# Outer product of routed experts: weights stationary instead of slots, with a turn back, in an eight-expert layer of a twelve-step network

## The chip, the cores and the metric

The kernel runs on one core of a Trainium2 chip. The metric is the time of one launch on the device in microseconds (us). A core has five engines that work from queues of their own: TensorE (PE; its weight loads are shown as PEld), VectorE (DVE), ScalarE (ACT), GpSimd (POOL) and SyncE (SP, which only starts transfers here). An engine takes its instructions strictly in order: an instruction that waits for a semaphore holds up everything behind it on its engine. All data here is fp32.

## The reference

Twelve steps work one after another on x, 4096 tokens of 128 numbers. Each adds a function of the normalised x to x:

```python
    x = L0_attn_x
    x = x + 0.5 * _L0_ffn_ref(_layernorm(x, axis=-1), ...)
    x = x + _L0_attn_ref(_layernorm(x, axis=-1), ...)
    x = x + 0.5 * _L0_ffn_ref(_layernorm(x, axis=-1), ...)
    x = x + 0.5 * _L1_ffn_ref(_layernorm(x, axis=-1), ...)
...
```

The layers L1, L2 and L3 follow in the same manner (ffn, attention, ffn). The change lies in `_L0_ffn_ref`, which is called twice. It is a layer of eight experts of which each token takes the two that its router prefers. Seven experts are real; the eighth only scales the token. Each real expert takes at most 512 tokens ("slots"):

```python
        cap = math.ceil(n_tok / n_exp * CAPACITY_FACTOR)
        logits = jnp.einsum('bsh,eh->bse', x, router_w) + router_b
        weights_flat = jax.nn.softmax(logits, axis=-1).reshape(n_tok, n_exp)
...
        inputs = inputs.reshape(cap, n_exp - 1, hidden)
        in_w = jnp.take_along_axis(expert_w, sorted_indices, axis=0)
        h = jax.nn.relu(jnp.einsum('ceh,ehi->cei', inputs, experts_inter))
        out = jnp.einsum('cei,eih->ceh', h, experts_out) * in_w[..., None]
        combined = jnp.zeros_like(x_flat).at[used_idx].add(out.reshape(-1, hidden))
        combined = combined + x_flat * (noop_w * noop_mask)[:, None]
```

So for each real expert there is an inner product, 512 slots x 128 by 128 x 512, then a relu, then an outer product, 512 slots x 512 by 512 x 128, then a factor for each slot, and then the slot's row is added to its token.

## The kernel before

**Stages.** `l0_block` runs the two feed-forward steps and the attention of layer 0. Each feed-forward step has three stages: routing (softmax, ranks within the experts, and two tables of row numbers, `src` and `dst`), the expert loop `experts` (L656), and the return, in which the experts' rows are read back and added to x (`returned`, L473). Routing stores the normalised tokens with their eight routing weights behind them as rows of 136 numbers in `xd`, in device memory. The first call of `experts` (L889) stands between the routing and the return with the attention; the second (L911) ends the block.

**Device memory.** Each call has an array of its own, `yds[n]`, with two rows for each token, one for each of its choices, and spare rows for empty slots. Rows that no expert writes must be zero, so `zeros(n)` (L464) writes them first: four transfers of 1 MB each, started by SyncE, from the tile z, which GpSimd fills with zeros once, at the kernel's start (L447). `zeros(0)` is issued among the weight loads. `zeros(1)` belongs to the second call and is issued in the first.

**The loop.** For each expert e of 7, with tiles of 128 partitions:
- fetch(e, s), s of 4: GpSimd gathers 128 rows of xd into the tile g (L664; four buffers, so four experts). Slots lie on partitions.
- turn(e): four transposes on TensorE (L676) put g's 128 columns on partitions, in gp; VectorE copies gp to gt (L678).
- inner(e): four matmuls (L684), for each a block of 128x128 of w1 stationary and gt's 512 columns (slots) moving. The results hp go through two PSUM banks; the relu to h is on VectorE for the odd ones (L686), on ScalarE for the even ones (L688). So h has the inner dimension on partitions and slots in columns.
- outer(e): 16 matmuls (L694): for each of four blocks of 128 slots, four blocks of the inner dimension are summed up in op. A block of h is stationary, and 128 columns of w2 move. The result has slots on partitions again, so the routing weight is one number per partition: ScalarE scales op to y with it, one activation for each block of slots (L697). y has three buffers.
- put(e, s): GpSimd scatters 128 rows of y into yds[n] (L668).

Three experts are fetched ahead of the loop. Then, for each e: inner(e), turn(e+1), outer(e), the four puts of e interleaved with the four fetches of e+3, and then the side work that falls to e.

**What sets the order.** Both calls run in a stretch in which the order of the program is the order of the instructions on TensorE, ScalarE and VectorE; in the first call also on SyncE (L887, L906). Elsewhere a planner places instructions. On GpSimd the order comes out as 16 gathers (experts 0 to 3), then put(0), fetch(4), put(1), fetch(5), put(2), fetch(6), and the puts of 3 to 6.

**Side work.** The list `beside` is spread over the seven experts: work k of m is done behind expert 7k // m. In the first call it is zeros(1), eight times self_part (four VectorE operations at L654: the eighth expert's share), and the loading of layer 1's weights (`l1_ffn_weights`, L990 to L1013, small loads on SyncE with some VectorE work; the first reader of one of them on another engine is at L1006). In the second call it is self_part in turn with eight steps that multiply layer 3's two weight matrices with each other (L1865, four matmuls of 128 columns into pp, and a ScalarE copy at L1866) and with small sums on VectorE for layer 2 (L1626, L1628). PSUM is shared by tags: "mm" (gp, op) and "hp" have two banks each, "f3" (pp) one.

**SyncE's queue in the first call.** zeros(1)'s four transfers stand first, then loads for later layers, then the loads r of yds[0] (L482), which wait for the scatters.

Of the kernel before, what the change touches and what calls it, by code (L numbers as in the profile page):

```python
# [8 lines left out]
F32 = mybir.dt.float32  # L9
I32 = mybir.dt.int32  # L10
AF = mybir.ActivationFunctionType
# [5 lines left out]
P = 128  # L17
NB = 8
# [126 lines left out]
class Net:  # L145
# [316 lines left out]
        return w  # L462

    def zeros(self, n):  # L464
        for k in range(4):
            self.nc.sync.dma_start(
                out=self.yds[n][2048 * k : 2048 * k + 2048, :].rearrange("(p n) d -> p (n d)", p=P), in_=self.z)
# [24 lines left out]
    def l0_block(self, w):  # L492
# [6 lines left out]
        nc, tc, a = self.nc, self.tc, self.a  # L499
        box = {}  # L500
        with ExitStack() as c:
# [149 lines left out]
            def self_part(b):  # L651
                for i in range(4):
                    t, x = 4 * b + i, self.x[b][:, i, :]
                    nc.vector.scalar_tensor_tensor(x, self.xn[b][:, i, :], box["pw"][:, t, 7:8], x, ALU.mult, ALU.add)  # L654

            def experts(wk, ps, n, beside):  # L656

                src, dst, yd = box["src"], box["dst"], self.yds[n]
                gs, gts, hs, ys = {}, {}, {}, {}

                def fetch(e, s):
                    if s == 0:
                        gs[e] = wk.tile([P, 4, P + 8], F32, tag="g", name="g", bufs=4)
                    nc.gpsimd.indirect_dma_start(  # L664
                        out=gs[e][:, s, :], out_offset=None, in_=self.xd[:, :], in_offset=bass.IndirectOffsetOnAxis(ap=src[:, e, s : s + 1], axis=0))

                def put(e, s):
                    put = nc.gpsimd.indirect_dma_start(  # L668
                        out=yd[:, :], out_offset=bass.IndirectOffsetOnAxis(ap=dst[:, e, s : s + 1], axis=0), in_=ys[e][:, s, :], in_offset=None)

                    self.apart(f"puts{n}", put.ins)

                def turn(e):
                    gp = ps.tile([P, 512], F32, tag="mm", name="gp")
                    for s in range(4):
                        nc.tensor.transpose(gp[:, s * P : (s + 1) * P], gs[e][:, s, 0:P], self.ident)  # L676
                    gts[e] = wk.tile([P, 512], F32, tag="gt", name="gt")
                    nc.vector.tensor_copy(gts[e], gp)  # L678

                def inner(e):  # L680
                    h = hs[e] = wk.tile([P, 4, 512], F32, tag="h", name="h")
                    for ic in range(4):
                        hp = ps.tile([P, 512], F32, tag="hp", name="hp")
                        nc.tensor.matmul(hp, lhsT=w["w1"][:, e, ic * P : (ic + 1) * P], rhs=gts[e], start=True, stop=True)  # L684
                        if ic % 2:
                            nc.vector.tensor_scalar(h[:, ic, :], hp, 0.0, None, ALU.max)  # L686
                        else:
                            nc.scalar.activation(h[:, ic, :], hp, AF.Relu)  # L688

                def outer(e):  # L690
                    op = ps.tile([P, 4, P], F32, tag="mm", name="op")
                    for s in range(4):
                        for ic in range(4):
                            nc.tensor.matmul(op[:, s, :], lhsT=hs[e][:, ic, s * P : (s + 1) * P], rhs=w["w2"][:, e, ic, :], start=(ic == 0), stop=(ic == 3))  # L694
                    y = ys[e] = wk.tile([P, 4, P], F32, tag="y", name="y", bufs=3)
                    for s in range(4):
                        nc.scalar.activation(y[:, s, :], op[:, s, :], AF.Copy, scale=gs[e][:, s, P + e : P + e + 1])  # L697

                for e in range(3):
                    for s in range(4):  # L700
                        fetch(e, s)
                turn(0)
                for e in range(7):
                    inner(e)
                    if e < 6:
                        turn(e + 1)
                    outer(e)
                    for s in range(4):
                        put(e, s)
                        if e + 3 < 7:  # L710
                            fetch(e + 3, s)
                    for k, work in enumerate(beside):
                        if k * 7 // len(beside) == e:
                            work()
# [171 lines left out]
                slots(bank)  # L886
            with tc.tile_pool(name="f0w", bufs=2) as wk, tc.tile_pool(name="f0e", bufs=2, space=PSUM) as ps, ordered(engines={*FIXED, mybir.EngineType.SP}):  # L887
                more = [lambda: box.__setitem__("w1", self.l1_ffn_weights(self.keep))]
                experts(wk, ps, 0, [lambda: self.zeros(1)] + [lambda b=b: self_part(b) for b in range(NB)] + more)  # L889
            with tc.tile_pool(name="f0m", bufs=2) as wk, tc.tile_pool(name="f0c", bufs=7, space=PSUM) as ps, ordered(engines=every):  # L890
                todo, bank = {}, banks(ps)
                load, both, add = self.returned(wk, self.yds[0], 3, True)
# [1 line left out]
                for g in range(4):  # L894
                    n = PACE * g
                    for k in range(2):
                        b = 2 * g + k
# [9 lines left out]
            with tc.tile_pool(name="f0w", bufs=2) as wk, tc.tile_pool(name="f0e", bufs=2, space=PSUM) as ps, ordered(engines=FIXED):  # L907
                w2, more = box["w2"]
                w3, steps = self.l3_ffn_weights(self.keep, wk, ps)
                parts = [lambda b=b: self_part(b) for b in range(NB)]  # L910
                experts(wk, ps, 1, [work for works in zip(parts, steps, more(ps)) for work in works] + [more(ps)[8]])  # L911
# [1131 lines left out]
```

## Time and profile before

| | |
|---|---|
| three timed runs | 2611.95, 2611.81, 2608.92 us; median 2611.81 |
| the profiled execution | 2632.98 us |
| its span, first to last instruction | 2631.2 us |
| mean granted TensorE clock | 0.96 |
| first call of the expert loop: first gather starts, last scatter has landed | 59.1, 145.3 us |
| second call | 273.1, 364 us |

The kernel is timed without the profiler; the profile comes from one further execution, with its own time. The span runs from the first to the last instruction; all positions in time count from its start. "Busy" is the time in which an engine executes an instruction other than waits and DMA starts. A row of the groups reads: line, engine, operation, out<-in by the names in the program, shapes, xcount | busy time in us, mean duration of one in ns | idle time of the engine just before them in us, and what released most of it. Busy time by stretch shows where in the kernel TensorE is not full (stretch in us, then busy time and number of instructions of each engine, mean granted clock, the share of time in which the DMA engines were busy, and GB/s):

```
40.00:59.00 19.00, 12.85 (x108) 11.27 (x107) 13.06 (x29) 1.35 (x4) 14.01 (x21) 1.00 0.56 163
59.00:145.00 86.00, 62.09 (x308) 40.93 (x308) 25.02 (x69) 15.81 (x42) 54.39 (x56) 0.84 0.24 72
145.00:273.00 128.00, 93.22 (x801) 73.32 (x801) 81.12 (x283) 59.93 (x188) 64.09 (x167) 0.83 0.22 59
273.00:364.00 91.00, 68.72 (x374) 47.70 (x374) 24.86 (x63) 17.60 (x50) 54.86 (x57) 0.90 0.31 88
364.00:2631.00 2267.00, 2121.45 (x16446) 1225.81 (x16446) 1855.12 (x5060) 1644.43 (x4069) 951.97 (x1670) 0.97 0.05 13
```

The columns of engines are PE, PEld, DVE, ACT and POOL. The two expert loops are the second and the fourth row.

### The profile page before, as it was taken

The page shows a single profiled execution, that of the slowest core. Times are in us where ns is not written, and L with a number is a line of the kernel's source. Part 1 is how long each engine was busy: PE and PEld are TensorE (multiplying, and loading weights), DVE is VectorE, ACT ScalarE, POOL GpSimd, SP SyncE. Part 2 cuts the span into 40 slices and gives each one's busy share as a digit, 9 for nine tenths or more (in the row PEclk, how much of TensorE's full clock was granted, in tenths as well). Part 3 has the DMA queues.
Part 4 walks back from the last instruction along what each step waited for, and adds up shares of the span by engine and source line. Part 5 has one row for each costly group of instructions (what it writes and reads, how often), then busy time and mean ns, then how long its engine had stood idle before and what let it go on. Part 6 is the DMA issues. An engine that isn't in the chain of part 4 may idle for free.

```text
span 2631.2 us, 51301 instructions
## 1 busy us (share of the span) xinstructions
PE 2389.5 (91%) x18184; PEld 1427.7 (54%) x18184; DVE 2024.7 (77%) x5597; ACT 1756.3 (67%) x4393; POOL 1154.0 (44%) x2003
## 2 busy tenths in 40 slices
PE   6858756999999998999999999999899999999997
PEld 6537533344444444566565655556565666666664
DVE  5347348888888866878788787877688989898897
ACT  2135134466677666766757676676598999999984
POOL 5655643244454452163452635332234545454443
PEclk9878877799999999999999999999899999999999
DMA  8121340001010100000000000000000000000000
GB/s 270 51 81 30 93 124 1 18 18 27 19 26 19 34 2 4 1 1 1 1 1 1 1 1 1 1 1 9 9 18 9 10 22 22 10 14 22 22 2 13
DMA packets 72962, 66.51 MB, mean 25 GB/s; under 512 B 15675, under 2 KB 62787, under 8 KB 70563
## 3 DMA queue, kind: packets, MB, share of 16 engines
q1 hardware_dynamic: 68096, 54.88, 7.7%
q0 software_dynamic: 3584, 7.58, 1.0%
q8 instruction: 145, 2.38, 0.4%
q10 hardware_dynamic: 1026, 0.78, 0.1%
q14 instruction: 111, 0.90, 0.1%
HBM read 36.47 MB, written 26.80 MB: 24 GB/s over the span
## 4 chain that ended last, share of the span: by engine, by line
PE 62%; DVE 20%; ACT 9%; POOL 4%; issue 3%; DMA 1%; another core or an unknown queue 0%; SPq 0%; POOLq 0%; DVEq 0%; ACTq 0%
PE tp L1476 8%; PE s L1450 6%; PE s L1290 5%; PE o L1757 4%; PE o L1492 4%; PE o L1320 4%; PE s L1706 4%; PE yp L384 3%; ACT e L1713 3%; PE s L1310 3%; DVE nm L1291 3%; DVE nm L1454 3%; PE tp L1732 2%; PE pp L1674 2%; PE hp L684 2%
## 5 line engine op out<-in xcount | busy, mean ns | idle before, releaser
L1461 ACT ACTIVATE e<-s,nm 128x512 f32<-128x512 f32 x512 | 345.4, 689 | 26.0 <-DVE nm L1454 21.4
L1291 DVE TENSOR_REDUCE nm<-s 128x2 f32<-128x1024 f32 x256 | 301.4, 1218 | 75.9 <-PE s L1310 61.0
L1454 DVE TENSOR_REDUCE nm<-s 128x2 f32<-128x1024 f32 x256 | 301.0, 1217 | 29.6 <-PE s L1450 27.7
L1482 ACT ACTIVATE p<-tp 128x512 f32<-128x512 f32 x512 | 279.3, 618 | 61.6 <-PE tp L1476 61.6
L1312 ACT ACTIVATE pr<-s 128x512 f32<-128x512 f32 x512 | 271.6, 600 | 73.1 <-PE s L1310 69.3
L1476 PE MATMUL tp<-cst,e 128*128 128x128 f32 x2048 | 294.3, 282 | 15.2 <-DVE rs L1467 7.9
L1476 PEld LDWEIGHTS tp<-cst,e 128*128 128x128 f32 x2048 | 221.5, 142 | 153.0 <-issue 86.8
L1470 POOL TENSOR_SCALAR e<-e,rs 128x512 f32<-128x512 f32 x114 | 200.1, 1755 | 229.8 <-DVE rs L1467 191.3
L1290 PE MATMUL s<-k,q 32*128 32x512 f32 x1024 | 279.2, 657 | 18.0 <-DVE nm L1291 14.6
L1310 PE MATMUL s<-q,k 32*128 32x512 f32 x1024 | 290.4, 627 | 5.4 <-DVE at L1333 4.4
L1713 ACT ACTIVATE e<-e,m 128x512 f32<-128x512 f32 (+3 forms) x512 | 286.1, 570 | 12.6 <-DVE m L1710 12.5
L1710 DVE CUSTOM_DVE_ANT_0 e<-s,bias 128x512 f32<-128x512 f32 (+3 forms) x512 | 220.1, 485 | 92.9 <-PE s L1706 92.4
L219 POOL TENSOR_TENSOR d<-st 128x4 f32<-128x4 f32 (+3 forms) x90 | 19.7, 218 | 554.2 <-DVE st L215 356.9
L1734 ACT COPY pt<-tp 128x512 f32<-128x512 f32 x320 | 174.5, 590 | 90.1 <-PE tp L1732 90.1
L386 DVE SCALAR_TENSOR_TENSOR x<-yp,sel,x 128x128 f32<-128x128 f32 x512 | 177.9, 348 | 39.7 <-PE yp L384 26.6
L1470 DVE TENSOR_SCALAR e<-e,rs 128x512 f32<-128x512 f32 x398 | 195.5, 521 | 9.1
L1743 DVE TENSOR_SCALAR e<-e,rc 128x512 f32<-128x512 f32 (+3 forms) x512 | 190.0, 416 | 9.1
L1732 PE MATMUL tp<-cst,e 128*128 128x128 f32 x1280 | 170.9, 278 | 9.8 <-ACT pt L1734 4.0
L1450 PE MATMUL s<-k,q 32*128 32x512 f32 x1024 | 174.8, 651 | 5.1 <-ACT e L1461 2.6
L1706 PE MATMUL s<-qk 64*128 64x512 f32 (+3 forms) x1024 | 173.6, 457 | 2.0 <-DVE m L1710 1.4
L1492 PE MATMUL o<-p,va 128*32 128x128 f32 x4096 | 165.8, 277 | 2.9 <-ACT p L1482 2.9
L1732 PEld LDWEIGHTS tp<-cst,e 128*128 128x128 f32 x1280 | 139.2, 141 | 48.5 <-issue 13.3
(467 smaller groups left out, 4848.0 us busy)
## 6 DMA issues: line engine op xcount, KB each, us to landing
yd<-z SPq DMA_DIRECT2D x8, 1024.0 KB
r<-yd SPq DMA_DIRECT2D x32, 256.0 KB
sk<-pu SPq DMA_DIRECT2D x16, 256.0 KB
k<-sk SPq DMA_DIRECT2D x60, 64.0 KB
w<-in_l_w SPq DMA_DIRECT2D x14, 256.0 KB
xd<-wqkv SPq DMA_DIRECT2D x12, 256.0 KB
x<-in_x SPq DMA_DIRECT2D x8, 256.0 KB
up<-in_l_up SPq DMA_DIRECT2D x8, 256.0 KB
```

What stands on the lines that cost most here:

```text
L1290: nc.tensor.matmul(s[:, jj, :], lhsT=q[cut, g, i * P : (i + 1) * P], rhs=k[cut, g, :], start=True, stop=True)
L1291: nc.vector.tensor_reduce(nms[b, g // 2][:, i, 2 * h : 2 * h + 2, g % 2], s, AX.X, ALU.max, negate=True)
L1310: nc.tensor.matmul(s, lhsT=k[cut, g, kt * P : (kt + 1) * P], rhs=q[cut, g, :], start=True, stop=True)
L1450: nc.tensor.matmul(s[:, jj, :], lhsT=q[cut, g, i * P : (i + 1) * P], rhs=k[cut, g, :], start=True, stop=True)
L1454: nc.vector.tensor_reduce(nm, scores[n, h], AX.X, ALU.max, negate=True)
L1461: nc.scalar.activation(e, s[:, jj, :], AF.Exp, bias=nm[:, jj : jj + 1], accum_out=sm[:, jj : jj + 1])
L1470: (nc.gpsimd if h and jj and n >= 14 else nc.vector).tensor_scalar(e, e, rc[:, jj : jj + 1], None, ALU.mult)
L1476: nc.tensor.transpose(tp[:, kt, :], probs[n][j][:, kt * P : (kt + 1) * P], self.ident)
L1482: nc.scalar.activation(p, turns[n].pop(0), AF.Exp)
L1706: nc.tensor.matmul(s[:, jj, 0:w], lhsT=qs[n][cut, i * P : (i + 1) * P], rhs=ks[n][cut, 0:w], start=True, stop=True)
L1713: outs.append(lambda e=e, jj=jj: nc.scalar.activation(e, e, AF.Exp, bias=mins[n][:, jj, i : i + 1], scale=-1.0, accum_out=sums[n][:, jj, i ...
L1732: nc.tensor.transpose(tp[:, k, :], block(n, jj, i, kt), self.ident)
```

## The change

- The outer product swaps its operands: a block of 128x128 of w2 is stationary and 512 columns of h (slots) move, four matmuls that are summed up in one bank op. The result has the model's 128 numbers on partitions and slots in columns. ScalarE copies it to the new tile ot.
- back(e) turns it back with four transposes into bp (a bank of the tag "mm"), and ScalarE scales bp to y, one activation for each block of slots as before.
- inner is cut into halves of two matmuls. The loop's order becomes: turn(0), inner(0), turn(1); then for each e: outer(e), first half of inner(e+1), back(e), second half of inner(e+1), puts and fetches as before, turn(e+2), side work.
- hp has three PSUM banks instead of two.
- zeros(1) moves from the first expert's side work to the third's (in the list: behind three self_parts), and ahead of its transfers VectorE sets one column of z to zero, which makes them wait for VectorE.

The same operations run on other data shapes; what is computed stays the same.

```diff
--- before.py
+++ after.py
@@ -462,6 +462,8 @@
         return w
 
     def zeros(self, n):
+        if n:
+            self.nc.vector.memset(self.z[:, 0:1], 0.0)
         for k in range(4):
             self.nc.sync.dma_start(
                 out=self.yds[n][2048 * k : 2048 * k + 2048, :].rearrange("(p n) d -> p (n d)", p=P), in_=self.z)
@@ -656,7 +658,7 @@
             def experts(wk, ps, n, beside):
 
                 src, dst, yd = box["src"], box["dst"], self.yds[n]
-                gs, gts, hs, ys = {}, {}, {}, {}
+                gs, gts, hs, ots, ys = {}, {}, {}, {}, {}
 
                 def fetch(e, s):
                     if s == 0:
@@ -677,10 +679,12 @@
                     gts[e] = wk.tile([P, 512], F32, tag="gt", name="gt")
                     nc.vector.tensor_copy(gts[e], gp)
 
-                def inner(e):
-                    h = hs[e] = wk.tile([P, 4, 512], F32, tag="h", name="h")
-                    for ic in range(4):
-                        hp = ps.tile([P, 512], F32, tag="hp", name="hp")
+                def inner(e, half):
+                    if not half:
+                        hs[e] = wk.tile([P, 4, 512], F32, tag="h", name="h")
+                    h = hs[e]
+                    for ic in (2 * half, 2 * half + 1):
+                        hp = ps.tile([P, 512], F32, tag="hp", name="hp", bufs=3)
                         nc.tensor.matmul(hp, lhsT=w["w1"][:, e, ic * P : (ic + 1) * P], rhs=gts[e], start=True, stop=True)
                         if ic % 2:
                             nc.vector.tensor_scalar(h[:, ic, :], hp, 0.0, None, ALU.max)
@@ -688,27 +692,40 @@
                             nc.scalar.activation(h[:, ic, :], hp, AF.Relu)
 
                 def outer(e):
-                    op = ps.tile([P, 4, P], F32, tag="mm", name="op")
+                    op = ps.tile([P, 512], F32, tag="mm", name="op")
+                    for ic in range(4):
+                        nc.tensor.matmul(op, lhsT=w["w2"][:, e, ic, :], rhs=hs[e][:, ic, :], start=(ic == 0), stop=(ic == 3))
+                    ot = ots[e] = wk.tile([P, 512], F32, tag="ot", name="ot")
+                    nc.scalar.copy(ot, op)
+
+                def back(e):
+                    bp = ps.tile([P, 4, P], F32, tag="mm", name="bp")
                     for s in range(4):
-                        for ic in range(4):
-                            nc.tensor.matmul(op[:, s, :], lhsT=hs[e][:, ic, s * P : (s + 1) * P], rhs=w["w2"][:, e, ic, :], start=(ic == 0), stop=(ic == 3))
+                        nc.tensor.transpose(bp[:, s, :], ots[e][:, s * P : (s + 1) * P], self.ident)
                     y = ys[e] = wk.tile([P, 4, P], F32, tag="y", name="y", bufs=3)
                     for s in range(4):
-                        nc.scalar.activation(y[:, s, :], op[:, s, :], AF.Copy, scale=gs[e][:, s, P + e : P + e + 1])
+                        nc.scalar.activation(y[:, s, :], bp[:, s, :], AF.Copy, scale=gs[e][:, s, P + e : P + e + 1])
 
                 for e in range(3):
                     for s in range(4):
                         fetch(e, s)
                 turn(0)
+                inner(0, 0)
+                inner(0, 1)
+                turn(1)
                 for e in range(7):
-                    inner(e)
+                    outer(e)
                     if e < 6:
-                        turn(e + 1)
-                    outer(e)
+                        inner(e + 1, 0)
+                    back(e)
+                    if e < 6:
+                        inner(e + 1, 1)
                     for s in range(4):
                         put(e, s)
                         if e + 3 < 7:
                             fetch(e + 3, s)
+                    if e < 5:
+                        turn(e + 2)
                     for k, work in enumerate(beside):
                         if k * 7 // len(beside) == e:
                             work()
@@ -886,7 +903,7 @@
                 slots(bank)
             with tc.tile_pool(name="f0w", bufs=2) as wk, tc.tile_pool(name="f0e", bufs=2, space=PSUM) as ps, ordered(engines={*FIXED, mybir.EngineType.SP}):
                 more = [lambda: box.__setitem__("w1", self.l1_ffn_weights(self.keep))]
-                experts(wk, ps, 0, [lambda: self.zeros(1)] + [lambda b=b: self_part(b) for b in range(NB)] + more)
+                experts(wk, ps, 0, [lambda b=b: self_part(b) for b in range(3)] + [lambda: self.zeros(1)] + [lambda b=b: self_part(b) for b in range(3, NB)] + more)
             with tc.tile_pool(name="f0m", bufs=2) as wk, tc.tile_pool(name="f0c", bufs=7, space=PSUM) as ps, ordered(engines=every):
                 todo, bank = {}, banks(ps)
                 load, both, add = self.returned(wk, self.yds[0], 3, True)
```

## The prediction

> **What bounds the kernel now.** I read the page's totals, then the two stretches in which the expert loop runs (59 to 145 us and 273 to 364 us): their groups by line, the timeline, the chain of waits.
>
> ```profile
> span 2631.2 us, 51301 instructions
> PE 2389.5 (91%) x18184; PEld 1427.7 (54%) x18184; DVE 2024.7 (77%) x5597; ACT 1756.3 (67%) x4393; POOL 1154.0 (44%) x2003
> ```
>
> TensorE is busy 91% of the span, but not in these two stretches: 62.3 of 89 us in the first, 68.7 of 91 us in the second (the busy times by stretch). The groups of the loop:
>
> ```profile
> L684 PE MATMUL hp<-gt,w 128*128 128x512 f32 x112 | 63.4, 700 | 15.3 <-ACT h L688 12.7 <-issue 1.6 <-DVE gt L678 0.8
> L668 POOL DMA_INDIRECT yd<-y,dst x56 | 54.6, 975 | 48.6 <-ACT y L697 35.1 <-issue 10.2 <-ACT h L688 2.7
> L694 PE MATMUL op<-w,h 128*128 128x128 f32 x448 | 53.5, 277 | 0.2
> L697 ACT ACTIVATE y<-op,g 128x128 f32<-128x128 f32 x56 | 16.0, 368 | 85.2 <-PE op L694 31.8 <-PE hp L684 28.4 <-remote 18.9
> ```
>
> The scatters (L668) wait for y, and y waits for the outer product. Why so long, the timeline of the first call shows (experts 2, 3 and 4):
>
> ```profile
> 96.79 3.80 PE L694 MATMUL op<-w,h 128*128 128x128 f32 x32
> 100.43 1.88 PE L684 MATMUL hp<-gt,w 128*128 128x512 f32 x4
> 102.31 0.94 POOL L664 DMA_INDIRECT g<-xd,src  x1 [0.30 <-issue]
> 105.40 1.14 ACT L697 ACTIVATE y<-op,g 128x128 f32<-128x128 f32 x4 [9.11 <-remote]
> 107.08 3.43 PE L684 MATMUL hp<-gt,w 128*128 128x512 f32 x4 [4.77 <-ACT h L688]
> ...
> 119.44 3.74 PE L694 MATMUL op<-w,h 128*128 128x128 f32 x32
> 123.21 1.14 ACT L697 ACTIVATE y<-op,g 128x128 f32<-128x128 f32 x4 [4.27 <-PE op L694]
> ...
> 130.92 1.14 ACT L697 ACTIVATE y<-op,g 128x128 f32<-128x128 f32 x4 [4.27 <-PE op L694]
> ```
>
> Expert 4: y starts 3.77 us after the outer product (123.21 - 119.44). Expert 2: 8.61 us, with the matmuls' records done by 100.6; TensorE then stands 4.77 us behind ScalarE and runs its next matmuls at a lower granted clock (0.68 from 105.5 to 110.8). The lateness over 3.77, expert by expert in the same view: first call 3.67, 0.56, 4.84, 0.94, then none; second call 5.36, 1.73, 1.78, 4.10, then none. Together 23.0 us, only in experts 0 to 3, the ones beside which gathers (L664) still run. Each call ends with its last scatter, so the lateness lies on the chain:
>
> ```profile
> 95.72 9.70 another core or an unknown queue
> ...
> 143.04 2.25 DMA yd<-y,dst
> ```
>
> The profiled execution took 2632.98 us (span 2631.2 and 1.8 around it), 21.2 us over the median 2611.81. That matters below.
>
> **The outer product.** Per expert 16 matmuls of 128 columns become 4 of 512. Row: 32 records at L694 take 3.57 us on the chain; two matmuls of L684's form take 1.72 (chain, 123.17), so four take 3.44: 0.13 less. New are four transposes back, priced by gp's four (0.44 on the chain), and a ScalarE copy of 128x512 (L1734's mean, 590 ns). TensorE's work per expert: inner 3.44, turn 0.44, outer 3.44, back 0.44 = 7.76. Before, an undisturbed expert took 130.92 - 123.21 = 7.71, with 0.28 us of standing in it. So in the steady state nothing is won: +0.05 x 14 = +0.7 us.
>
> [...] The trace has 112 ns and 430 ns a record, in proportion to the columns, for this fp32 form; the row decides.
>
> **Order, banks, latency.** back(e) stands between the halves of inner(e+1), and waits for the copy: the copy needs 0.59 us, the first half covers 1.72. If a completion comes over 1.13 us late, TensorE waits there, and behind it queue the second half, the next turn and the next outer. Three inner banks remove the stand behind ScalarE (0.28, counted above). y comes later after the outer product by the half inner, 0.44 back and about 0.2; for the last expert, which has no half to interleave, by 0.59 + 0.44 + 0.1 = 1.14. ScalarE gains 7 copies of 0.59 per call on 2.34 us of work in each 7.7; hidden. DVE: one memset of one column (the 128x1 rows are 0.15), hidden.
>
> **Zeros later.** Three of the four 1 MB writes of zeros(1) start at 54.35, just before the first gathers; the DMA engines are 97% busy from 54 to 66 us (busy times by stretch), and the first gather takes 6.39 us to land:
>
> ```profile
> 59.14 6.39 DMA g<-xd,src
> ...
> 276.99 2.56 DMA g<-xd,src
> ```
>
> In the second call, without zeros, the gather takes 2.56. GpSimd issues expert 0's fourth gather at 63.20, so it can land at 65.76 where its transpose now starts at 67.63: TensorE starts 1.87 earlier. The zeros now wait for the memset behind DVE's gt of expert 4 (expert 2's turn, near 97 us); behind them on SyncE stand only ten small loads of layer 1's weights, first read at 135.23 (L1006), and the loads of yd, which wait for the scatters. Cover of about 30 us; if it were gone, some 8 us (12 issues of 0.4 to 1.3). The writes then meet gathers of experts 5 and 6: between 0 and 6.39 - 2.56 = 3.8 us; these have one expert of slack, I take 1.5.
>
> **What sets the end afterwards.** Call 1, GpSimd: 16 gathers end at 79.13, then 28 scatters x 1.28 and 12 gathers x 1.26 (durations of L668, L664 plus the 0.30 between them) = 50.9, so 130.4 at best. TensorE: outer(0) at 74.85 - 1.87 = 72.98, outer(6) 6 x 7.76 later at 119.5, y at 119.5 + 3.44 + 1.14 + 0.2 = 124.3, last scatter over 0.64 + 5.1 later at 130.0. GpSimd sets it: 144.0 now, 130.4 + 1.5 then: 12.1 less. Call 2: outer(0) stays at 286.65 and each expert carries 0.89 of L1865: 286.65 + 6 x 8.65 + 3.44 + 1.34 + 5.74 = 349.1; GpSimd alone 344.8; now 362.3: 13.2 less. Sum 25.3 us, if the lateness goes. I think it does in the trace: matmuls of 512 columns beside the same gathers are answered at once (ScalarE's h at 71.14 and 73.57), only the dense blocks of 128 columns are not.
>
> How much of it is in runs without the profiler no row tells. From both sides: all of it (25.3), or the profile's whole excess over the median is this lateness and only 25.3 - 21.2 = 4.1 is left. Neither end is nearer by a row, so the middle, 14.7: **2611.8 - 14.7 = 2597.1 us**, own range 2586.5 to 2607.7. The profiled span itself should be near 2606.
>
> [...]
>
> **Rivals.**
> *Only the profiled execution is late* (same). For: the lateness, 23.0, is about the excess, 21.2. Against: the excess could lie anywhere in 2.6 ms; nothing but the like size ties it to these eight experts. Then call 1 is GpSimd's queue in both kernels (130.4 before too), and call 2 gains nothing and pays 7 x 0.05 + 1.14 = 1.5: 2613.3 us.
>
> *Two hand-offs are late instead of one* (slower). Place: experts 0 to 3 of both calls, ScalarE's copy of the outer product and then y. If lateness belongs to any completion of TensorE while gathers run, its mean, 23.0 / 8 = 2.87 us, strikes the copy too; 1.13 is covered, 1.74 is not: 8 x 1.74 = 13.9, less the 1.87 of the earlier start, plus 2 x 1.14: 2626. It decides from 1.13 us per hand-off on. For: at 121.21 the copy gt waits 1.32 "remote" with no dense block before it. Against: hp's completions beside the same gathers.
>
> *Zeros over the gathers* (slower, or same): 3.8 us for each of experts 5 and 6 in call 1, nothing won elsewhere: 2611.8 + 7.6 + 1.5 - 1.87 = 2619.
>
> **How the numbers follow.** Chances: forecast 0.55, only profiled 0.25, two hand-offs 0.13, zeros 0.07. Less than 0.2% (5.2 us) can't be told from no change. The forecast's range ends 4.1 us below the median, but mostly lies beyond 5.2: faster 0.55; the first rival is the same: 0.25; the two others slower: 0.20. The range reaches from 2584 (all 25.3 and 2.5 for clocks that stay full) to 2620, past the first rival and the zeros, and leaves out the two hand-offs.
>
> **What would show it.** Right: in experts 0 to 3 too, y (L707) starts within 1 us of the end of its transposes back, no "remote" before L707 or L699, call 1 ending near 132 and call 2 near 349, first transposes done by 66.5. If the span falls by 25 us and the time by less than 5, the first rival holds. Idle time of TensorE before bp (L704) behind the copy is the second. Gathers of experts 5 and 6 landing over 5 us after issue, with TensorE waiting at L678, is the third. The forecast is wrong if y stays late, whatever the shape of the matmuls.

## The result: no difference that counts

The changed kernel takes 2614.26 us (median of 20 runs, 2610.17 to 2620.61), the kernel before 2609.55 us (20 runs, 2605.79 to 2613.94). The ratio is 1.0019, 95% interval [1.0011, 1.0028]: 3 to 7 us slower, inside the 0.2% that was named as the bound of no change. The forecast was 2597.1 and faster. The profiled execution took 2611.59 us, and it is one of the 20 runs, near their lower end. Every timed run comes with a span and a granted clock of its own. So being profiled is not what set the first profile (2632.98) apart from the runs beside it.

The page's totals and the groups of the loop in the profile after:

```profile
span 2609.8 us, 50763 instructions
...
PE 2381.3 (91%) x17904; PEld 1398.7 (54%) x17904; DVE 2023.7 (78%) x5598; ACT 1762.6 (68%) x4407; POOL 1151.5 (44%) x2003
```

```profile
L688 PE MATMUL hp<-gt,w 128*128 128x512 f32 x112 | 56.4, 632 | 1.7 <-DVE gt L680 1.7
...
L670 POOL DMA_INDIRECT yd<-y,dst x56 | 55.6, 993 | 24.6 <-ACT y L707 9.9 <-issue 9.1 <-ACT h L692 1.8
...
L697 PE MATMUL op<-h,w 128*128 128x512 f32 x112 | 50.4, 593 | 0.0
...
L707 ACT ACTIVATE y<-bp,g 128x128 f32<-128x128 f32 x56 | 16.0, 368 | 9.3 <-PE bp L704 8.6 <-DMA yd<-y,dst 0.6
...
L704 PE MATMUL bp<-cst,ot 128*128 128x128 f32 x56 | 8.5, 274 | 1.5 <-ACT ot L699 1.5
L699 ACT COPY ot<-op 128x512 f32<-128x512 f32 x14 | 8.2, 585 | 53.5 <-PE op L697 53.5
```

Against the first profile all looks as forecast: GpSimd stands 24.6 us before the scatters (L670) instead of 48.6, of it 9.9 behind y instead of 35.1; TensorE no longer stands behind ScalarE at L688; the span is 21.4 us shorter. Experts 1 and 2 in the timeline of the first call:

```profile
81.12 3.60 PE L697 MATMUL op<-h,w 128*128 128x512 f32 x8
...
84.56 1.88 PE L688 MATMUL hp<-gt,w 128*128 128x512 f32 x4
...
86.27 0.60 PE L704 MATMUL bp<-cst,ot 128*128 128x128 f32 x4
...
86.91 1.14 ACT L707 ACTIVATE y<-bp,g 128x128 f32<-128x128 f32 x4 [0.64 <-PE bp L704]
...
88.87 3.60 PE L697 MATMUL op<-h,w 128*128 128x512 f32 x8
```

An expert takes 88.87 - 81.12 = 7.75 us, and y starts 0.04 us after bp's end. But the time did not fall. So the question was at once whether the kernel before, in the runs that were timed, had any of the lateness that this profile lacks.

### The profile page after: what moved, and what is told of

Its sections match the earlier page's. It is cut to its first block, busy times and chain, and to the rows that moved or that the text cites. A ratio compares the mean times of both kernels' runs of the same rounds, so it can differ in the third digit from the quotient of the medians.

```text
span 2609.8 us, 50763 instructions
## 1 busy us (share of the span) xinstructions
PE 2381.3 (91%) x17904; PEld 1398.7 (54%) x17904; DVE 2023.7 (78%) x5598; ACT 1762.6 (68%) x4407; POOL 1151.5 (44%) x2003
## 4 chain that ended last, share of the span: by engine, by line
PE 56%; DVE 16%; ACT 7%; POOL 3%; issue 2%; POOLq 0%; ACTq 0%; DVEq 0%
PE tp L1493 8%; PE s L1467 6%; PE s L1307 5%; PE o L1509 4%; PE o L1337 4%; PE o L1774 4%; PE s L1723 4%; PE yp L384 3%; DVE nm L1308 3%; PE s L1327 3%; ACT e L1730 3%; DVE nm L1471 3%; PE tp L1749 2%; PE pp L1691 2%; DVE e L1727 2%; PE op L1783 2%
## 5 line engine op out<-in xcount | busy, mean ns | idle before, releaser
L1329 ACT ACTIVATE pr<-s 128x512 f32<-128x512 f32 x512 | 271.5, 601 | 73.6 <-PE s L1327 69.9
```

## The experiments

Six groups of runs, each on one chip with the kernel before beside the variants; ratios are against it, with 95% intervals. Edits are against the kernel before or the changed one, as said. Two kinds of chip came up: in the result's runs and on chips 9 and 12 the kernel before has medians of 2609.6 to 2612.6 us (no run of it over 2617.7), on chips 1 and 15 of 2643.6 to 2644.7 (none under 2635.6). I call the first kind prompt and the second late. Which chip a group gets is not chosen; chips 1 and 15 came up twice each and were late both times.

On which chip the first profile (2632.98 us) was taken is not known, but its trace shows the kind. The traces record events on eight semaphores that go with the 112 indirect transfers of the two calls (56 gathers and 56 scatters). The seven traces of prompt chips with these transfers hold 1780 to 1807 events on the eight, about 16 for each transfer, which would be 1792; the ten of late chips hold 741 to 835. The first profile holds 784, the same kernel on chip 9 has 1797. So the first profile is of the late kind, although its 2632.98 us lie a little below all 88 runs of the kernel before on chips 1 and 15.

### The parts, on a prompt chip

**The kernel before, profiled again.**

> The kernel before, unchanged, profiled once more and timed against itself. Theory 1 (the lateness belongs to the profiled execution): timed ratio 1.000, and no timed run near 2633. If profiling such a kernel always brings it, the new profile again takes 2625 to 2640 us, with y (L697) 4 to 10 us behind the outer product in experts 0 to 3 of both calls and the calls ending near 144 and 362 us. If it was one disturbed execution, the new profile takes 2606 to 2615 us, y starts 3.8 us behind the outer product in all 14 experts, and the calls end near 133 and 340 us. Theory 2 (the lateness is in every run, and the changed kernel loses 25 us elsewhere): the new profile shows the lateness and takes as long as the timed runs, 2606 to 2614 us.

Ratio 1.0003 [0.9992, 1.0015]. The profiled execution took 2613.71 us, in the middle of the timed ones. The timeline, experts 2 and 3 of the first call and the last scatter:

```profile
91.34 3.74 PE L694 MATMUL op<-w,h 128*128 128x128 f32 x32
...
95.12 1.14 ACT L697 ACTIVATE y<-op,g 128x128 f32<-128x128 f32 x4 [4.27 <-PE op L694]
...
99.06 3.74 PE L694 MATMUL op<-w,h 128*128 128x128 f32 x32
...
102.83 1.14 ACT L697 ACTIVATE y<-op,g 128x128 f32<-128x128 f32 x4 [4.27 <-PE op L694]
...
130.45 0.97 POOL L668 DMA_INDIRECT yd<-y,dst  x1 [0.30 <-DMA yd<-y,dst]
```

y starts 3.78 us behind the outer product while gathers run, and 7.71 us lie between experts: the same kernel, with its dense blocks of 128 columns, without any lateness. Its calls take 71.5 and 76.0 us from the first gather's start to the last scatter's end; the changed kernel's 72.9 and 77.6, measured alike. So on such a chip each call became 1.4 to 1.6 us longer.

**The changed kernel, zeros early.**

```diff
     def zeros(self, n):
-        if n:
-            self.nc.vector.memset(self.z[:, 0:1], 0.0)
...
-                experts(wk, ps, 0, [lambda b=b: self_part(b) for b in range(3)] + [lambda: self.zeros(1)] + [lambda b=b: self_part(b) for b in range(3, NB)] + more)
+                experts(wk, ps, 0, [lambda: self.zeros(1)] + [lambda b=b: self_part(b) for b in range(NB)] + more)
```

> The changed kernel with the zeros written early, where the kernel before has them, and without the memset. The changed kernel measured 1.0019 of before. If the small loss comes from zeros that meet the gathers of later experts, this gains it back: ratio 0.999 to 1.0005. If it comes from the outer product and the turn back, the zeros are worth nothing or the 1.87 us of the earlier first transpose: ratio 1.002 to 1.003. In the profile the first transposes end near 68 us, not 66.5.

Ratio 1.0020 [1.0009, 1.0032]: the place of the zeros is not the loss. Call 1 takes 73.2 us against 72.9.

**The kernel before, zeros late:** the same edit the other way round.

> The kernel before with only the zeros moved. If the zeros cost the loss: ratio 1.0015 to 1.003 and gathers of experts 5 and 6 that land over 4 us after their issue. If the move is neutral: 0.999 to 1.0005. Theory 1 expects nothing of the 10 to 25 us of lateness to show in the times either way.

Ratio 1.0008 [0.9997, 1.0018]: between the two expectations, and not told from neutral. What the move gives and takes can be seen in the changed kernel's timeline:

```profile
66.05 0.47 PE L678 MATMUL gp<-cst,g 128*128 128x128 f32 x1 [0.78 <-DMA g<-xd,src]
...
97.61 0.06 DVE L466 MEMSET z<- 128x1 f32 x1
97.71 3.09 SPq L468 DMA_DIRECT2D yd<-z  x4
...
106.09 0.33 PE L678 MATMUL gp<-cst,g 128*128 128x128 f32 x1 [0.93 <-DMA g<-xd,src]
106.26 3.60 PE L697 MATMUL op<-h,w 128*128 128x512 f32 x8
```

The first transposes are done at 66.52, as said (66.5), 7.1 us after the first gather's start; in the kernel before, profiled again, it is 9.2 us (69.11 - 59.90). The zeros, issued at 97.71, then hold up expert 5's gathers: the transpose waits until 106.09, and outer(4) starts at 106.26, 9.65 us after outer(3) at 96.61, 1.9 more than the 7.75 of the others. One gather took 7.0 us to land where the median is 2.5. The gain at the start is given back here.

**The changed kernel with the outer product of before** (order, three banks and late zeros stay):

```diff
 def outer(e):
-    op = ps.tile([P, 512], F32, tag="mm", name="op")
-    for ic in range(4):
-        nc.tensor.matmul(op, lhsT=w["w2"][:, e, ic, :], rhs=hs[e][:, ic, :], start=(ic == 0), stop=(ic == 3))
-    ot = ots[e] = wk.tile([P, 512], F32, tag="ot", name="ot")
-    nc.scalar.copy(ot, op)
+    op = ps.tile([P, 4, P], F32, tag="mm", name="op")
+    for s in range(4):
+        for ic in range(4):
+            nc.tensor.matmul(op[:, s, :], lhsT=hs[e][:, ic, s * P : (s + 1) * P], rhs=w["w2"][:, e, ic, :], start=(ic == 0), stop=(ic == 3))
...
-                    back(e)
```

> The changed kernel with the outer product of before (16 matmuls of 128 columns, slots stationary, no copy, no turn back); new order of the loop, three inner banks, zeros late. If the loss comes from the swapped outer product with its copy and turn back (0.05 us per expert and 1.14 us at each call's end, by my sum 3 us): ratio 0.999 to 1.0008. If from order, banks or zeros: 1.0015 to 1.003. If dense blocks of 128 columns answer late whenever gathers run, its profile shows y late in experts 0 to 3 and TensorE, which now has the next inner product ahead of nothing that waits for y, running on.

Ratio 1.0006 [0.9996, 1.0016]. In its second call, outer(3) and outer(2) are 300.92 - 292.58 = 8.34 us apart, against 8.64 in the changed kernel (302.44 - 293.80) and 8.60 in the kernel before (301.85 - 293.25): the new order and banks are worth 0.26 us per expert, the swapped outer product with its turn back costs 0.30. The second call takes 73.6 us here, 77.6 in the changed kernel. So by these profiles the swapped outer product is the price, and the order with three banks had paid most of it. The times alone don't show it: the interval overlaps that of the changed kernel, 1.0011 to 1.0028, and though the second call is 2.3 us shorter here than in the kernel before (76.0), the ratio is not under 1.

### What is late, on a late chip

**Half of the outer product left out of the kernel before** (`for ic in (0, 3)` in outer).

> The kernel before with half of the outer product left out (two of the four blocks of the inner dimension), 1.79 us of TensorE less per expert; the output is not the reference's. If GpSimd's queue of 28 gathers and 28 scatters sets a call's length (71 us at 1.27 us each) and TensorE is only beside it: call 1 stays at 71.5 us, call 2 falls from 76.0 to 71.5, ratio 0.998 to 0.999. If TensorE sets both calls: 12.5 us less in each, ratio near 0.990.

This group ran on a late chip: ratio 0.9990 [0.9979, 1.0001]. 25 us less of TensorE's work (14 x 1.79) bring 0 to 6 us, so on this kind of chip the calls wait for something else.

**The changed kernel, turn back at once** (back(e) moved ahead of the first half).

> The changed kernel with the turn back directly behind the outer product instead of between the halves of the next inner product. The wait for ScalarE's copy is then open on TensorE: about 0.73 us per expert, what the last expert shows, 4.4 us per call, ratio 1.004 to 1.0055. If each hand-off from TensorE were late by 2.9 us beside gathers, as in the first profile, experts 0 to 3 would pay that besides: 1.012 and more. If GpSimd's queue hides it: no more than 1.003.

1.0027 [1.0013, 1.0040], less than the 1.004 to 1.0055 expected, against 1.0000 for the changed kernel itself on the other late chip (below). TensorE stands 0.73 us at bp behind the copy even where no gather runs, in experts 5 and 6. The interleaving does hide the copy.

**The changed kernel with two inner banks** (`bufs=3` taken out).

> The changed kernel with two PSUM banks for the inner product instead of three. If the third bank is what takes away the 0.28 us that TensorE stood behind the relu: 0.28 us more per expert, ratio 1.0025 to 1.0035. If the turn back between the halves already gives the relu that time: as the changed kernel, 1.0015 to 1.0025.

0.9996 [0.9984, 1.0007]. On a late chip the time alone couldn't show 0.28 us per expert, but two experts without a late result can: outer(3) and outer(4) are 7.75 us apart (116.66 - 108.91), as with three banks. So the third bank brings nothing there, since the turn back between the halves already gives the relu its time.

**The changed kernel without copy and turn back** (y from op's columns; not the reference's output).

> The changed kernel without ScalarE's copy and without the turn back: y is scaled straight from op, whose columns are slots, so the output is not the reference's. What is left is the swapped outer product alone. If the copy and the turn back are the loss: about 0.44 us per expert and 1.3 us at the end less in call 2, call 2 near 73 us instead of 77.6, call 1 held at 71.3 by GpSimd, ratio 0.999 to 1.0005. If the loss is elsewhere: 1.0015 to 1.0025.

0.9978 [0.9966, 0.9991], the lowest of this group, 0.22% or 5.8 us under the changed kernel's 1.0000 on the other late chip. Expected were 4.4 us (7 x 0.44 + 1.3, in the second call alone). If the two late chips are alike, copy and turn back cost at least what was summed.

**The changed kernel again.**

> The changed kernel, unchanged, once more. Two conditions have been seen: chips on which the kernel before takes 2610 us and TensorE's results are never late, and one on which it takes 2644 us and they are late beside the gathers, as in the first profile. On a chip of the first kind: ratio 1.001 to 1.003, as measured. On one of the second kind, the forecast's mechanism (512 columns are answered at once) expects 15 to 25 us less, ratio 0.990 to 0.995; the rival of two late hand-offs expects 1.000 to 1.006, with ScalarE's copy (L699) 2 to 5 us late in experts 0 to 3.

A late chip (before 2644.7): 2643.67, ratio 1.0000 [0.9991, 1.0009]. This is the rival's lower end; the 15 to 25 us of the forecast's mechanism are not there. Expert 2 in its timeline:

```profile
91.52 3.60 PE L697 MATMUL op<-h,w 128*128 128x512 f32 x8
94.95 1.88 PE L688 MATMUL hp<-gt,w 128*128 128x512 f32 x4
98.68 0.58 ACT L699 COPY ot<-op 128x512 f32<-128x512 f32 x1 [7.49 <-remote]
99.32 0.66 PE L704 MATMUL bp<-cst,ot 128*128 128x128 f32 x4 [2.49 <-issue]
...
105.70 1.14 ACT L707 ACTIVATE y<-bp,g 128x128 f32<-128x128 f32 x4 [3.61 <-PE gp L678]
```

The copy starts 7.16 us after the outer product (98.68 - 91.52), where the prompt chip has 3.64 (84.76 - 81.12, expert 1), and y follows 5.72 us after the end of bp. Matmuls of 512 columns are late as well, in two hand-offs instead of one. The calls take 87.0 and 90.8 us, 27 us more than on the prompt chip; the rest of the kernel is hardly longer (the spans differ by 29.8).

**The kernel before without the gathers of experts 3 to 6.**

```diff
                 def fetch(e, s):
+                    if e > 2:
+                        gs[e] = gs[e - 3]
+                        return
```

> The kernel before without the gathers of experts 3 to 6, which work on the rows of experts 0 to 3 again, so the output is not the reference's; the scatters stay. On a chip with lateness: if the gathers bring it, it stays in expert 0 at most, and the kernel takes 20 to 33 us less, ratio 0.988 to 0.992; if something else in these stretches brings it, 0.999 to 1.001. On a chip without: TensorE and GpSimd end a call together in the kernel before, so the same calls of 71.5 and 76 us, ratio 0.999 to 1.000, although GpSimd has 15 us less to do per call.

Same late chip: 2610.12, ratio 0.9869 [0.9852, 0.9885]. All of the lateness is gone; experts 2 and 3 of the first call:

```profile
90.48 3.74 PE L697 MATMUL op<-w,h 128*128 128x128 f32 x32
...
94.26 1.14 ACT L700 ACTIVATE y<-op,g 128x128 f32<-128x128 f32 x4 [4.27 <-PE op L697]
94.90 0.97 POOL L671 DMA_INDIRECT yd<-y,dst  x1 [2.92 <-ACT y L700]
```

y is 3.78 us behind again. And though GpSimd now waits before every group of scatters (2.92), call 1 takes 71.6 us, as on the prompt chip (71.5): TensorE's seven experts alone need that long, and the 16 gathers less for GpSimd (20 us at 1.25 each, not the 15 of the expectation) gain nothing.

**Plain loads of as many bytes in their place.**

```diff
+                    if e > 2:
+                        nc.sync.dma_start(out=gs[e][:, s, :], in_=self.xd[(4 * e + s) * P : (4 * e + s + 1) * P, :])
+                        return
```

> The kernel before with the gathers of experts 3 to 6 replaced by plain loads of as many bytes, started by SyncE (consecutive rows, so the output is not the reference's). On a chip with lateness: if the bytes that arrive beside TensorE's work bring it, the time stays, 0.999 to 1.001; if GpSimd's making of the gathers brings it, 20 to 33 us less, 0.988 to 0.992. On a chip without: as without the gathers, 0.999 to 1.000.

0.9886 [0.9871, 0.9901]. Here too y starts 3.77 us behind each outer product (81.42 - 77.65, and so on), while the loads are started, between 82.6 and 99.8. The bytes are not it; the indirect gather is.

**Rows of 512 B** (the array seen as rows of 128 numbers) and **consecutive rows** (an index table in order), in the kernel before.

> The kernel before with gathers of 128 numbers a row (512 B) instead of 136 (544 B), from the same array read as rows of 128; the routing weight is left out and a number of the row stands in for it, so the output is not the reference's. On a chip with lateness: if the row length of 544 B brings it, ratio 0.985 to 0.990; if any gather does, 0.998 to 1.001. On a chip without: 0.999 to 1.001.

> The kernel before with gathers of consecutive rows: the index table holds rows in order instead of the experts' tokens (one VectorE operation more, and the output is not the reference's). On a chip with lateness: if scattered rows bring it, ratio 0.985 to 0.990; if it is the gather as such, 0.998 to 1.001. On a chip without: 0.999 to 1.001.

1.0003 [0.9987, 1.0020] and 1.0011 [0.9994, 1.0028] on a late chip: neither the row's length nor the scattered reads bring it.

**All gathers first**, in the kernel before:

```diff
-                        gs[e] = wk.tile([P, 4, P + 8], F32, tag="g", name="g", bufs=4)
+                        gs[e] = wk.tile([P, 4, P + 8], F32, tag="g", name="g", bufs=7)
...
-                for e in range(3):
+                for e in range(7):
                     for s in range(4):
                         fetch(e, s)
...
-                        if e + 3 < 7:
-                            fetch(e + 3, s)
```

> The kernel before with all 28 gathers issued ahead of the loop and seven buffers for them; nothing else changed. On a chip with lateness: the last gather is issued 35 us after the first instead of 60, so experts 3 to 6 run undisturbed and at most the first two or three are late: each call 5 to 10 us shorter, ratio 0.992 to 0.997. If the lateness goes with each gather made beside TensorE's work and not with the stretch: no gain, 0.999 to 1.001. On a chip without: GpSimd's queue is as long as before, 0.999 to 1.001.

Slower: 1.0060 [1.0039, 1.0080], outside both expectations. The miss shows the thing best:

```profile
76.68 3.74 PE L694 MATMUL op<-w,h 128*128 128x128 f32 x32
...
93.89 0.94 POOL L664 DMA_INDIRECT g<-xd,src  x1 [0.30 <-issue]
99.97 1.14 ACT L697 ACTIVATE y<-op,g 128x128 f32<-128x128 f32 x4 [24.14 <-remote]
100.05 0.69 DVE L686 TENSOR_SCALAR h<-hp 128x512 f32<-128x512 f32 x1 [21.27 <-remote]
...
101.64 2.93 PE L684 MATMUL hp<-gt,w 128*128 128x512 f32 x3 [18.76 <-ACT h L688]
```

The outer product has run by 80.4 by its records, but y starts at 99.97, 5.1 us after the last of the gathers has ended (94.83). VectorE gets its results of TensorE no earlier (100.05), and TensorE stands 18.76 us for want of ScalarE's h, which waits for TensorE; the turn of expert 2, whose last gather ended on GpSimd at 74.87, stands behind it. In the second call TensorE itself is held up as well. Behind the outer product stand small matmuls of the side work, then the next inner product; the last four of the former and the first four of the latter come one by one, 1.4 to 2.8 us apart, with idle time that nothing in the profile explains:

```profile
305.47 0.37 PE L1863 MATMUL pp<-down,up 128*128 128x128 f32 x1 [2.53 <-issue]
308.26 0.37 PE L1863 MATMUL pp<-down,up 128*128 128x128 f32 x1 [2.42 <-issue]
```

So it is not only the notice of a result that comes late.

**The changed order with the old outer product and early zeros.**

> The changed kernel's order and its three banks, with the outer product of before and the zeros at the old place: no copy, no turn back. On a chip without lateness: the stand of 0.28 us per expert is gone and call 2 is 2 us shorter, call 1 is held by GpSimd, ratio 0.9985 to 0.9998, the fastest of the variants. On a chip with lateness: TensorE has the next inner product to do while y is late, and the gain is as large or larger, 0.995 to 0.9995. If the order gains nothing: 1.000 to 1.001.

1.0009 [0.9989, 1.0028] on a late chip: no gain from order and banks there.

**The changed kernel with all gathers first** (the edit above), on two chips.

> The changed kernel with all 28 gathers ahead of the loop and seven buffers for them. On a chip with lateness the kernel before, so treated, had no y before 99.97 us and took 1.006. If the forecast's mechanism holds in part (512 columns are answered beside gathers, dense blocks of 128 are not): the first y near 80 to 85 us, experts 1 to 6 follow at 7.75 us once the gathers have ended at 95 us, each call 5 to 10 us shorter than in the changed kernel, ratio 0.992 to 0.997. If any result of TensorE waits for a burst of gathers to end: the first copy (L699) near 99 us, ratio 1.004 to 1.008. On a chip without lateness: 1.001 to 1.003, as the changed kernel.

1.0015 [0.9999, 1.0031] on the prompt chip, as the changed kernel.

> The changed kernel with all gathers first once more, since the last run was on a chip without lateness. The same expectations: on a chip with lateness 0.992 to 0.997 with the first y near 80 to 85 us if 512 columns are answered beside gathers, 1.004 to 1.008 with the first copy near 99 us if any result of TensorE waits; on a chip without, 1.000 to 1.003.

On a late chip 1.0037 [1.0024, 1.0049]:

```profile
72.56 3.60 PE L697 MATMUL op<-h,w 128*128 128x512 f32 x8
...
77.40 0.58 ACT L699 COPY ot<-op 128x512 f32<-128x512 f32 x1 [5.35 <-PE hp L688]
78.04 0.66 PE L704 MATMUL bp<-cst,ot 128*128 128x128 f32 x4 [0.17 <-issue]
...
90.77 1.14 ACT L707 ACTIVATE y<-bp,g 128x128 f32<-128x128 f32 x4 [9.96 <-remote]
```

The copy was answered (4.84 us, 1.2 late), the turn back was not: y starts 12 us after it, though 3.3 us before the last gather has ended (94.06). So neither expectation held: the copy didn't wait for the burst, and y came later than 85. Which hand-off waits differs with the shape of the outer product; that something waits doesn't.

**Scatters in the place of the gathers** (16 indirect writes of h's rows to an unread array, in the kernel before).

> The kernel before with each of the 16 gathers of experts 3 to 6 replaced by a scatter of 128 rows of h to an array that nothing reads; experts 3 to 6 work on the rows of experts 0 to 2 again, so the output is not the reference's. GpSimd makes as many indirect transfers as before, and writes as many bytes. On a chip with lateness: if indirect transfers as such bring it, 0.998 to 1.002; if only gathers do, 0.985 to 0.990, as with plain loads. On a chip without: 0.999 to 1.001.

1.0006 [0.9995, 1.0018], on the prompt chip, so it doesn't tell. That scatters alone do no harm at their usual pace is seen in the run without late gathers, where all 28 scatters of a call stayed (ratio 0.9869, y 3.78 us behind); whether a dense burst of them would is open.

## Why the prediction was wrong

*What bounds the kernel.* The lines were read rightly in the main: in that execution y was late only beside gathers, and the scatters, and with them each call's end, followed from it. (Of the 23.0 us, the 0.56 of expert 1 is no lateness: its matmuls took 4.29 us instead of 3.74, and y followed them within 0.04.) It was not true of the runs that set the median. On a chip with the times of those runs, the same kernel has calls of 71.5 and 76.0 us and no lateness.

*The step that failed:* "Neither end is nearer by a row, so the middle, 14.7". This is the term for the gain that the timed runs would see. On that kind of chip there is none, and the change costs 3 to 7 us: below both ends. A row that was nearer stood beside it: the three runs lie within about 3 us, the profiled execution 21.2 above them, and the lateness found in it, 23.0, is about that excess. With it the sum would have been made against the undisturbed calls, which is the first rival: 2613.3, against 2614.26 measured. That rival's number is luck in part, and its reason was wrong. It gave the loss of 1.5 us to the second call alone, where the profiles show 1.4 and 1.6 in the two calls. And it was not the profiled execution that was late but the chip: on chips 1 and 15 all 88 runs of the kernel before take over 2635 us.

*"Only the dense blocks of 128 columns are not"* answered at once: also false, so that the forecast fails on a late chip too. It is shown by the changed kernel there (copy 3.5 us late in expert 2) and by the turn back held for 12 us. A row of the first profile spoke against it already: VectorE's relu L686 of two matmuls of 512 columns that start at 100.43 stands at 105.54, 5.1 us later, where it is 2.0 on the prompt chip (96.89 - 94.92). The second rival had the place right, two hand-offs that are late, but not the size: it had 14 us more than before, and the late chip shows a ratio of 1.0000 [0.9991, 1.0009]. So the number of late hand-offs doesn't set the loss. How long each is held is not worked out; single profiles on late chips differ by 3 us in a call (kernels that differ only in what the gathers read: 87.0 and 90.0 in call 1).

*The terms that held.* Outer product 3.44 (81.12 to 84.56) and turn back 0.44 (86.27 to 86.71), both as summed; copy 585 ns (590), hidden but in the last expert, where TensorE stands 0.73 us; 7.75 us per expert (7.76). The last y comes 5.02 us after its outer product's start (126.84 - 121.82), summed 4.78; in the kernel before 4.15 (125.92 - 121.77). The early start was 2.0 us instead of 1.87 (from the first gather to outer(0): 14.0 us, 16.0 in the kernel before), the collision of the zeros 1.9 + 0.5 instead of 1.5. These two nearly cancel, which fits the two runs on the zeros' place. Call 1 was summed to end at 131.9 and ended at 132.3; call 2, counted from its first gather, 76.0 and 77.6.

*What the small loss is made of.* Per call 7 x 0.04 for the expert and 0.9 for the last y, 1.2, against 1.4 and 1.6 in the profiles: together 3.0 us, at the near end of the measured 3 to 7. The rest was not pinned down: one profile of each kernel can't do it where the runs spread over 10 us.

*Faster version.* None was found: no variant that computes the reference is under 1.0 beyond its interval on either kind of chip.

## What to carry to other kernels

When the profiled execution is longer than every timed run, find out first whether the stall that you mean to remove is the excess; if the two are alike in size, build the sum on the timed runs and profile the kernel once more, on another chip, before changing it. Before a late result is put down to the shape of the work that makes it, take the neighbour away in one run: here the run without the gathers told what no rearrangement of the matmuls could. Where two queues end a stage together (here GpSimd's 56 indirect transfers of 1.27 us and TensorE's seven experts), work taken from one of them alone need not gain anything: 20 us less on GpSimd's queue left call 1 at 71.6 us.

## What the runs showed of the hardware

- On two of the four chips of the experiments TensorE's results reach ScalarE and VectorE late while GpSimd issues indirect gathers: up to 20 us with a burst of 28 (outer product done at 80.4, y at 99.97). The kernel takes 33 us more there (2644 against 2611); without late gathers 2610 on the same chip. Plain loads of the same bytes don't do it (2612). In the burst TensorE's own matmuls come up to 2.8 us apart. Why these chips and not others is not settled.
- On the same two chips the trace lacks events. The eight semaphores of the indirect transfers have 741 to 835 of some 1792, and TensorE's completion semaphore has 3420 where the same program (the changed kernel) has 3462 on a prompt chip, with the whole shortfall inside the two loops. But missing events are not a sign of late results: the run without late gathers, with no lateness, lacks as many of TensorE's (3363 against 3406 of the kernel before on chip 9) and has 712 of 1280 on the eight. So the loss of events marks the chip. Whether it has a cause in common with the late results is not shown.
- In the first profiles of the two kernels the granted TensorE clock is 1.00 or 0.50 in every record, at places that differ between the two executions: from 20 to 40 us, ahead of the loop, its mean was 0.57 in the changed kernel and 1.00 in the kernel before, with the same work (83 matmuls, 16.2 and 16.6 us busy).
